# Cross-attention softmax divided on the query rows, and one layer's mask added to the copied scores by GpSimd

## The chip, the cores and the metric

The kernel runs on one core of one Trainium2 chip. Such a core has a TensorE for matrix products, three engines for elementwise work (VectorE or DVE, ScalarE or ACT, GpSimd or POOL) and a SyncE that issues most of the transfers. They share a memory of 128 partitions, SBUF, and the matmuls write into a second one of eight banks, PSUM. Each engine takes its instructions in order and waits at semaphores for the others. The metric is the device time of one execution in microseconds; lower is better.

## The reference, cut to what matters

Two transformer layers on 2 sequences of 1024 rows with 256 columns; each has self-attention, cross-attention to a context of 64 rows, and a feed-forward part. Layer 0's feed-forward is a mixture of 8 experts of which each row takes 2. Layer 1's is dense, and its cross-attention has a mask on the keys. All is float32, with 16 heads of 16 columns. The cross-attention of layer 1 reads:

```python
q = _heads(xn @ q_w.T)
k = _heads(codebook_embeds @ k_w.T)
v = _heads(codebook_embeds @ v_w.T)
attn = jnp.einsum('bhnd,bhmd->bhnm', q, k) * SCALE          # 1024 rows x 64 keys per head
bias = (1.0 - codebook_mask.astype(attn.dtype))[:, None, None, :] * -10000.0
attn = jax.nn.softmax(attn + bias, axis=-1)
ca = _merge(jnp.einsum('bhnm,bhmd->bhnd', attn, v)) @ ca_proj_w.T
x = x + ca
```

Layer 0's has the same form without `bias`. A softmax is: the row's maximum, the difference, the exponential, the sum over the row, and the division by it. The division can be made on the weights or, since the product with v is linear, on the product.

## The kernel before

**Self-attention.** Each layer goes through 128 cells (function `self_attention`). A cell multiplies four tiles of scores of 128x512 with queries on partitions, only for their row maxima (the "a" scores, L801, reduced by DVE at L808), ten cells ahead (`LEAD`), and four with keys on partitions (the "b" scores, L812), which ACT turns into exponentials `pt_s` (L818). Every two cells the product with v follows (L863); ACT copies it (L875) and GpSimd adds it up (L876). So "beside the maxima" below means: while cells with both kinds of scores run. In the last ten cells of a layer there are no "a" scores any more.

**The planner.** All other work is a task, a generator that issues some instructions and yields their estimated TensorE time in us; a yield of zero or less asks for a pause of so many us, which the planner rounds up to cells of 2.9 us, at least one (`Stream.advance`). In each cell the planner takes steps of tasks up to a paced amount. After the last cell, `Stream.rest` orders what is left by rank and by these times. The result fixes the order of instructions on PE, DVE, ACT and SP; GpSimd's order comes from it by way of the scheduler.

**Cross-attention.** The 2048 rows go in four blocks of 512 (`cross_tasks`). For each there are three tasks: `norm`, `weigh`, `share`. `weigh` handles the 16 heads in two groups of eight, and each group in four tiles of 128x512: on the partitions are 128 queries, and in the row four query tiles t, two heads and 64 keys, so that a tile holds 128x8 rows of 64 scores. Its steps are named by two letters:

- SC, `scores`: for two tiles, eight matmuls (L1138), in layer 1 with eight more ahead of them that write the mask into the bank from one row of ones (L1129). Beside the maxima ACT copies the bank to SBUF (`sc_c`, L1149). Otherwise DVE takes maximum and difference straight from the bank.
- LA, `largest`: beside the maxima, DVE's maximum of the copied tile (L1158, 128x8 maxima) and GpSimd's subtraction (L1159).
- TU, `weights_turned`: TensorE transposes two tiles (L1174), and ACT takes the exponential from the bank (`pt_c`, L1178); keys are now on partitions.
- PR, `product`: four matmuls with v (L1187) into one bank; 16 with a matrix of zeros and ones from `picks` into another, which gives the sums over keys (L1197); ACT copies the product to `q_c`, DVE takes the reciprocal of the sums (L1206, 128x128, `inv_c`).
- DI, `divided`: four matmuls spread the reciprocals over the columns of each head (L1212), and DVE multiplies `q_c` by them (L1219).

`share` waits, makes the second DI and projects onto the rows (L433). A step that runs once `maxima[0]` is false, after the last "a" scores, takes the other form: this holds for block 3 and a part of block 2 in layer 0, and for blocks 2 and 3 in layer 1. There the list of steps is written out with a pause for each.

**Around it.** In layer 0 the mixture's dispatch (L1424 and others) runs beside the last cells; expert slots are TensorE work from 590 to 950 us (L1651, L1681), with ACT's Gelu at L1657. Their results leave by indirect transfers (L1696). The last slots are under a run-time condition (`Mixture.others`), at the joint where layer 1's cells begin. The slots' weights (`slotw`) and other tiles (`epool`) lie in pools that are closed at this joint; layer 1's tiles take their places. At the end of layer 1 the feed-forward (L1811, L1823, Gelu at L1814) is all that stands beside the last cross blocks.

Of the kernel before, what the change touches and what calls it, by code (L numbers as in the profile page):

```python
# [50 lines left out]
P = 128  # L51
B, S, D, H, DH = 2, 1024, 256, 16, 16
SK = 64
# [53 lines left out]
O_SUM, O_HEAD = 0, 128  # L107

O_ROWS, O_PART = 640, 704
NPICK = 768  # L110
# [91 lines left out]
def two_blocks(  # L202
# [100 lines left out]
    def other_constants():  # L303
        nc.gpsimd.memset(restart, 1.0)
        nc.gpsimd.memset(restart[:, :, 0:1], 0.0)
        nc.gpsimd.memset(vbds[0], 0.0)

# [214 lines left out]
    def self_attention(layer, tail, heads, arrive, extra, when_ready, beside=None):  # L522
# [379 lines left out]
        if layer == 0:  # L902
# [9 lines left out]
            for _ in first_heads():  # L912
                pass
            stream.add(biases(), 3.3, last=6, mark="biases")
# [183 lines left out]
    def weigh(layer, b, pool, w, name, held):  # L1098
# [24 lines left out]
        def scores(g, n):  # L1123

            got = [(r, *bank()) for r in (2 * n, 2 * n + 1)]
            for t in range(4):
                for r, _, p in got if layer == 1 else ():
                    at = slice(32 * r, 32 * r + 1)
                    nc.tensor.matmul(  # L1129
                        p[:, t * P : (t + 1) * P].rearrange("p (u k) -> p u k", k=SK),  # L1130
                        lhsT=ones[at, :],
                        rhs=mask_f[at, b * SK : (b + 1) * SK].unsqueeze(1).to_broadcast([1, 2, SK]),
                        start=True,
                        stop=False,
                    )
                for r, _, p in got:
# [5 lines left out]
                        start=(layer == 0),  # L1142
# [20 lines left out]

        def largest(g, r):
            if (g, r) in whole_scores:
                subtract(less[g, r], less[g, r], nc.gpsimd, f"{g}{r}")

        def weights_turned(g, n):

            for r in (2 * n, 2 * n + 1):  # L1170
# [7 lines left out]
                nc.scalar.activation(pt, p, AF.Exp, scale=SCALE)  # L1178
                free.append(i)


        inverse = {}

        def product(g):
# [9 lines left out]
            j, s = bank()  # L1194
            for r in range(4):
                for c in range(4):
                    nc.tensor.matmul(  # L1197
                        s[32 * c : 32 * (c + 1), :P],
                        lhsT=picks[:, O_SUM + 32 * r : O_SUM + 32 * (r + 1)],
                        rhs=pts[g, r][:, c * P : (c + 1) * P],  # L1200
                        start=(r == 0),
                        stop=(r == 3),
                    )
            nc.scalar.copy(q[:, g, :], o)
            inv = inverse[g] = pool.tile([P, P], F32, tag="inv", name=f"inv_{name}{g}", bufs=2)
            nc.vector.reciprocal(inv, s[:, :P])  # L1206
            free.extend((i, j))

        def divided(g):
            i, p = bank()  # L1210
            for c in range(4):
                nc.tensor.matmul(  # L1212
                    p[:, c * P : (c + 1) * P],
                    lhsT=picks[:, O_HEAD + c * P : O_HEAD + (c + 1) * P],
                    rhs=inverse[g],
                    start=True,
                    stop=True,
                )
            nc.vector.tensor_tensor(q[:, g, :], q[:, g, :], p, ALU.mult)  # L1219
            free.append(i)  # L1220

        held.update(ot=q, divided=divided)
        cost = 1.9 if layer else 1.0
        SC, LA, TU, PR, DI = scores, largest, weights_turned, product, divided
        if maxima[0]:

            for now, wait in (
                (((SC, 0, 0), (LA, 0, 0)), 0.0),
                (((LA, 0, 1),), 0.0),
                (((SC, 0, 1), (LA, 0, 2)), 0.0),  # L1230
                (((TU, 0, 0), (LA, 0, 3)), 0.0),
                (((SC, 1, 0), (LA, 1, 0)), 0.0),
                (((TU, 0, 1), (LA, 1, 1)), 0.0),
                (((SC, 1, 1), (LA, 1, 2)), 0.0),
                (((PR, 0), (LA, 1, 3)), -1.5),
                (((TU, 1, 0),), None),
                (((DI, 0), (TU, 1, 1)), -1.4),
                (((PR, 1),), None),
            ):
                for step, *args in now:  # L1240
                    step(*args)
                us = sum({SC: cost, TU: 1.15, PR: 1.1, DI: 0.55}.get(step[0], 0.0) for step in now)
                if us:
                    yield us
                if maxima[0]:
                    yield 0.0
                elif wait is not None:
                    yield wait
            return
        for step, *args, wait in (  # L1250
            (SC, 0, 0, None),
            (SC, 0, 1, -1.0),
            (TU, 0, 0, None),
            (SC, 1, 0, None),
            (TU, 0, 1, -1.3),
            (PR, 0, None),
            (SC, 1, 1, None),
            (TU, 1, 0, None),
            (DI, 0, None),
            (TU, 1, 1, -1.6),  # L1260
            (PR, 1, None),
        ):
            step(*args)
            yield {SC: cost, TU: 1.15, PR: 1.1, DI: 0.55}[step]
# [3 lines left out]
    def share(w, name, first, held):  # L1268

        yield -2.6  # L1270
        held["divided"](1)
        yield 0.55
        yield -1.2
# [670 lines left out]
    slotw.append(slots.enter_context(tc.tile_pool(name="slotw", bufs=2, side="right")))  # L1944
    for n in range(2):
        epool.append(
            slots.enter_context(tc.tile_pool(name=f"epool{n}", bufs=2 - n, side="right"))
        )
    mixture.load()
# [31 lines left out]
    def beside(begin):  # L1981
# [4 lines left out]
        both.rest({}, 0)  # L1986
        mixture.others()
# [18 lines left out]
def _layout(inputs):  # L2006
# [84 lines left out]
    for r in range(4):  # L2091
        for u in range(2):
            for c in range(4):
                picks[SK * u : SK * (u + 1), O_SUM + 32 * r + 8 * c + 2 * r + u] = 1.0
# [52 lines left out]
```

## Time and profile before

| | us |
|---|---|
| three runs | 1619.12, 1614.07, 1609.81 |
| their median | 1614.07 |
| the profiled execution | 1624.94 |
| its span in the trace | 1623.2 |
| layer 0's cells | about 54 to 589 |
| layer 1's cells | about 956 to 1462 |

Times are read from the start of the span. A line such as "L1178 ACT ACTIVATE pt_c<-banks 128x512 ... x64 | 35.4, 612 | 22.1 <-PE banks L1174" says: 64 activations at line 1178, from PSUM ("banks") to `pt_c`, busy 35.4 us in all and 612 ns each; ACT stood idle for 22.1 us just before them, mostly until the transposes of L1174 had come. A float32 matmul of the program stands as two records, so that the 16 sum matmuls of a group are 32 of L1197. Matmuls overlap, so their number by their mean may exceed their busy time. In a row of a stretch come its limits and length, then busy time and instructions of each engine, the granted TensorE clock (1.00 is full), the transfers' share and their GB/s. In the chain of waits a row has the time, the duration and the work: it follows the last instruction back to what released each step.

### The profile page before, as it was taken

How to read it: one execution, taken by the hardware profiler on the slowest of the kernel's cores; microseconds unless marked ns; L12 is line 12 of the kernel's file. 1: busy time of each engine (PE TensorE's matmuls, PEld its weight loads, DVE VectorE, ACT ScalarE, POOL GpSimd, SP SyncE). 2: the span in 40 equal slices, each digit the busy share in tenths (PEclk: the TensorE clock that was granted, in tenths of full speed). 3: DMA queues.
4: the chain of work that ended last, by engine and by line, in shares of the span. 5: the costliest groups of instructions: out<-in, count | busy, mean ns of one | idle time of the engine just before them, and what ended most of it. 6: DMA issues, size and time to landing. Idle time of an engine off the chain costs nothing.

```text
span 1623.2 us, 28319 instructions
## 1 busy us (share of the span) xinstructions
PE 1579.5 (97%) x10710; PEld 876.8 (54%) x10710; DVE 985.1 (61%) x2094; ACT 912.9 (56%) x1767; POOL 411.0 (25%) x546
## 2 busy tenths in 40 slices
PE   7999999999998999999999999999999999999998
PEld 3433444544443547878888653344344435546766
DVE  5787776687778647511114457876867767855400
ACT  3487777676665755332233327876776676674321
POOL 2243323144235202311112032411322323311000
PEclk9899999999998999999999999999999999999999
DMA  5235311101000115375556321101110002000000
GB/s 158 112 133 194 111 27 34 28 21 47 14 21 34 54 50 196 102 275 188 186 201 217 92 72 27 33 23 21 34 33 21 22 14 83 15 14 21 14 13 26
DMA packets 55751, 121.07 MB, mean 75 GB/s; under 512 B 12218, under 2 KB 26428, under 8 KB 55228
## 3 DMA queue, kind: packets, MB, share of 16 engines
q1 hardware_dynamic: 51772, 109.07, 20.7%
q0 software_dynamic: 3456, 9.51, 1.6%
q8 instruction: 86, 1.41, 0.4%
q10 hardware_dynamic: 384, 0.66, 0.2%
q14 instruction: 53, 0.43, 0.1%
HBM read 71.68 MB, written 38.88 MB: 68 GB/s over the span
## 4 chain that ended last, share of the span: by engine, by line
PE 89%; DVE 7%; ACT 1%; issue 1%; DMA 1%; another core or an unknown queue 1%; POOL 0%; SPq 0%; DVEq 0%; POOLq 0%; ACTq 0%
PE banks L812 16%; PE banks L801 14%; PE banks L863 13%; PE banks L1651 8%; PE banks L1681 8%; PE banks L631 4%; PE banks L433 3%; PE banks L1823 3%; PE banks L1811 3%; DVE mx_s L808 3%; PE banks L1138 2%; PE banks L601 2%; PE banks L1174 2%; PE banks L1108 2%; PE banks L365 2%; PE banks L709 1%
## 5 line engine op out<-in xcount | busy, mean ns | idle before, releaser
L808 DVE TENSOR_REDUCE mx_s<-banks 128x1 f32<-128x512 f32 x1024 | 634.7, 682 | 215.3 <-PE banks L801 210.3
L818 ACT ACTIVATE pt_s<-banks 128x512 f32<-128x512 f32 x1024 | 532.6, 609 | 155.7 <-PE banks L801 124.8
L801 PE MATMUL banks<-KS,QS 16*128 16x512 f32 x2048 | 537.4, 631 | 4.0 <-DVE count L1441 2.6
L812 PE MATMUL banks<-qb_s,KS 32*128 32x512 f32 x2048 | 517.6, 623 | 6.7 <-DVE qb_s L711 3.7
L876 POOL TENSOR_TENSOR acc_s<-acc_s,part_s 128x512 f32<-128x512 f32 x141 | 179.5, 1273 | 439.0 <-ACT part_s L875 438.3
L812 PEld LDWEIGHTS banks<-qb_s,KS 32*128 32x128 f32 x2048 | 181.0, 187 | 178.5 <-DVE mx_s L808 105.4
L863 PE MATMUL banks<-pt_s,v_s 128*20 128x512 f32 x2048 | 262.0, 603 | 1.5 <-DVE mx_s L808 1.0
L801 PEld LDWEIGHTS banks<-KS,QS 16*128 16x128 f32 x2048 | 200.9, 186 | 76.3 <-issue 37.0
L1681 PE MATMUL banks<-w_slot,h_s 128*128 128x256 f32 x640 | 143.3, 380 | 2.7 <-ACT h_s L1657 2.7
L863 PEld LDWEIGHTS banks<-pt_s,v_s 128*20 128x20 f32 x2048 | 43.0, 98 | 185.0 <-ACT pt_s L818 131.6
L1681 PEld LDWEIGHTS banks<-w_slot,h_s 128*128 128x128 f32 x640 | 120.5, 190 | 22.8 <-ACT h_s L1657 3.1
L875 ACT COPY part_s<-banks 128x512 f32<-128x512 f32 x155 | 92.7, 598 | 61.3 <-PE banks L863 50.6
L1690 DVE SCALAR_TENSOR_TENSOR ys<-banks,gate,b 128x256 f32<-128x256 f32 x40 | 19.3, 483 | 170.3 <-PE banks L1681 163.3
L1657 ACT ACTIVATE h_s<-banks,w_slot 128x256 f32<-128x256 f32 x104 | 43.7, 471 | 109.0 <-issue 61.9
L1651 PE MATMUL banks<-xsT,w_slot 128*128 128x256 f32 x416 | 95.4, 381 | 0.7 <-ACT xsT L372 0.7
L1696 POOL DMA_INDIRECT results<-ys,to x40 | 38.8, 970 | 225.8 <-DVE ys L1690 183.3
L1651 PEld LDWEIGHTS banks<-xsT,w_slot 128*128 128x128 f32 x416 | 77.4, 190 | 14.9 <-DVE mx_s L808 2.3
L1159 POOL TENSOR_TENSOR sc_c<-sc_c,mx_c 128x512 f32<-128x512 f32 x38 | 40.0, 1054 | 98.8 <-DVE mx_c L1158 98.7
L631 PE MATMUL banks<-xT_s,w_att 128*128 128x512 f32 x128 | 63.9, 635 | 0.0
L1814 ACT ACTIVATE h_f<-banks,w_ff 128x512 f32<-128x512 f32 x32 | 22.0, 687 | 73.9 <-PE banks L1811 73.9
L1657 ACT ACTIVATE h_s<-banks,spare 128x256 f32<-128x256 f32 x56 | 23.3, 471 | 63.9 <-issue 30.4
L1823 PE MATMUL banks<-w_ff,h_f 128*128 128x256 f32 x256 | 57.3, 380 | 0.0
(270 smaller groups left out, 1647.2 us busy)
## 6 DMA issues: line engine op xcount, KB each, us to landing
w_slot<-in_ff_w_dram SPq DMA_DIRECT2D x40, 576.0 KB
sorted_rows<-fill SPq DMA_DIRECT2D x36, 520.0 KB
w_slot<-in_ff_w_dram SPq DMA_DIRECT2D x26, 514.0 KB
whole<-acc_s SPq DMA_DIRECT2D x30, 256.0 KB
spare<-in_ff_w_dram SPq DMA_DIRECT2D x14, 514.0 KB
xs<-sorted_rows SPq DMA_DIRECT2D x20, 260.0 KB
y<-results SPq DMA_DIRECT2D x16, 256.0 KB
QS<-stq_s SPq DMA_DIRECT2D x124, 32.0 KB
```

Of the source, the lines that this page charges most:

```text
L631: nc.tensor.matmul(p, lhsT=w[:, at + k * D + pair * P : at + k * D + (pair + 1) * P], rhs=xT[b][:, k, blk * 512 : (blk + 1) * 512], start= ...
L801: nc.tensor.matmul(sc, lhsT=QS[h % 4][r, qc * P : (qc + 1) * P], rhs=K[r, kh * 512 : (kh + 1) * 512], start=True, stop=True,)
L808: return i, lambda: nc.vector.tensor_reduce(mx[h][:, qc, j, kh : kh + 1], sc, AX.X, ALU.max)
L812: nc.tensor.matmul(sc, lhsT=K[r, n * P : (n + 1) * P], rhs=QB[h][r, :], start=True, stop=True)
L818: nc.scalar.activation(pt, sc, AF.Exp, scale=SCALE)
L863: nc.tensor.matmul(o[32 * j : 32 * j + VW, :], lhsT=V[b][:, cell % 8, 4 * g + j, :], rhs=exps.pop((cell, j)), start=(cell == cells[0]), st ...
L875: nc.scalar.copy(part, o)
L876: helper().tensor_tensor(acc[h], acc[h], part, ALU.add)
L1651: nc.tensor.matmul(ph[:, n, :], lhsT=w[:, at : at + P], rhs=xT[:, k, :], start=(k == 0), stop=(k == 1),)
L1657: nc.scalar.activation(h1[:, f, :], ph[:, n, :], AF.Gelu, bias=w[:, W_B1 + f : W_B1 + f + 1])
L1681: nc.tensor.matmul(py, lhsT=h1[:, f, h * P : (h + 1) * P], rhs=w[:, f * D : (f + 1) * D], start=(f == 0), stop=(f == 7),)
L1823: nc.tensor.matmul(py[:, n, :], lhsT=h1[:, f, t * P : (t + 1) * P], rhs=w2[:, f * D : (f + 1) * D], start=(f == 0), stop=(f == 7),)
```

## The change

The exponential moves ahead of the transposes, so that queries are still on partitions when the weights are summed. Four things follow:

- EX, `exponentials`: ACT takes the exponential of a subtracted tile in SBUF, in place. TU's activation becomes a copy.
- DI, `divided`, is another step than before: DVE's sum over each row of 64 keys (128x8 sums), their reciprocals, and the product of tile and reciprocals, by GpSimd beside the maxima and by DVE after them. The matmuls of L1197 and L1212, the reciprocals of 128x128 and the products of L1219 go, and with them a sixth of `picks`. `share` has no DI any more, and waits once.
- MA, `mask`: in layer 1, beside the maxima, the mask is added to the copied scores by GpSimd, ahead of their maximum, and the matmuls of L1129 are left out. After the maxima they stay.
- The order beside the maxima is now computed: one tile per cell, SC every second one; with MA, LA one cell later; EX two cells after LA, DI one after EX, TU and PR behind. It has 15 cells in layer 0 and 17 in layer 1, for 11 entries before. The list for after the maxima has new pauses too.

Two edits lie outside: `epool` is opened before `slotw`, and two activations of one column (`ready_for_exp`) take an exponential ahead of its use, one near the start of layer 0, one ahead of the conditional slots.

```diff
-O_SUM, O_HEAD = 0, 128
-
-O_ROWS, O_PART = 640, 704
-NPICK = 768
+O_HEAD = 0
+
+
+O_ROWS, O_PART = 512, 576
+NPICK = 640
...
+    def ready_for_exp():
+
+        nc.scalar.activation(root, eps, AF.Exp)
+
...
             for _ in first_heads():
                 pass
+            ready_for_exp()
             stream.add(biases(), 3.3, last=6, mark="biases")
...
             got = [(r, *bank()) for r in (2 * n, 2 * n + 1)]
+            masked = layer == 1 and not maxima[0]
             for t in range(4):
-                for r, _, p in got if layer == 1 else ():
+                for r, _, p in got if masked else ():
...
-                        start=(layer == 0),
+                        start=not masked,
...
+        def mask(g, r):
+            if (g, r) in whole_scores:
+                sc = less[g, r].rearrange("p (c k) -> p c k", k=SK)
+                row = mask_f[:, b * SK : (b + 1) * SK].unsqueeze(1).to_broadcast(shape)
+                nc.gpsimd.tensor_tensor(sc, sc, row, ALU.add)
+
         def largest(g, r):
             if (g, r) in whole_scores:
                 subtract(less[g, r], less[g, r], nc.gpsimd, f"{g}{r}")
+
+        def exponentials(g, r):
+            nc.scalar.activation(less[g, r], less[g, r], AF.Exp, scale=SCALE)
+
+        def divided(g, r):
+
+            sc = less[g, r].rearrange("p (c k) -> p c k", k=SK)
+            sm = pool.tile([P, 8], F32, tag="smc", name=f"sm_{name}{g}{r}", bufs=4)
+            nc.vector.tensor_reduce(sm, sc, AX.X, ALU.add)
+            nc.vector.reciprocal(sm, sm)
+            helper().tensor_tensor(sc, sc, sm.unsqueeze(2).to_broadcast(shape), ALU.mult)
 
         def weights_turned(g, n):
...
-                nc.scalar.activation(pt, p, AF.Exp, scale=SCALE)
+                nc.scalar.copy(pt, p)
                 free.append(i)
...
+        costs = {scores: 1.9 if layer and not maxima[0] else 1.0, weights_turned: 1.15, product: 0.55}
...
         if maxima[0]:
...
+            m = layer
+            cells = [[] for _ in range(15 + 2 * m)]
+            for k in range(8):
+                g, r = divmod(k, 4)
+                at = k + (2 + m) * g
+                if r % 2 == 0:
+                    cells[at].append((SC, g, r // 2))
+                    cells[at + 5 + m].append((TU, g, r // 2))
+                if m:
+                    cells[at].append((MA, g, r))
+                cells[at + m].append((LA, g, r))
+                cells[at + m + 2].append((EX, g, r))
+                cells[at + m + 3].append((DI, g, r))
+            for g in range(2):
+                cells[9 + m + (5 + m) * g].append((PR, g))
+            for now in cells:
                 for step, *args in now:
                     step(*args)
-                us = sum({SC: cost, TU: 1.15, PR: 1.1, DI: 0.55}.get(step[0], 0.0) for step in now)
+                us = sum(costs.get(step, 0.0) for step, *_ in now)
                 if us:
                     yield us
...
+                if now is not cells[-1]:
+                    yield 0.0 if maxima[0] else -1.5
             return
...
+        for now, wait in (
+            (((SC, 0, 0),), None),
+            (((SC, 0, 1),), -2.0),
+            (((EX, 0, 0), (EX, 0, 1)), -1.2),
+            (((DI, 0, 0), (DI, 0, 1), (EX, 0, 2), (EX, 0, 3)), -2.4),
+            (((TU, 0, 0), (DI, 0, 2), (DI, 0, 3)), None),
+            (((SC, 1, 0),), -1.6),
+            (((TU, 0, 1),), -1.0),
+            (((SC, 1, 1), (PR, 0)), -1.6),
+            (((EX, 1, 0), (EX, 1, 1)), -1.2),
+            (((DI, 1, 0), (DI, 1, 1), (EX, 1, 2), (EX, 1, 3)), -2.4),
+            (((TU, 1, 0), (DI, 1, 2), (DI, 1, 3)), -2.6),
+            (((TU, 1, 1),), -1.6),
+            (((PR, 1),), None),
         ):
...
     def share(w, name, first, held):
 
-        yield -2.6
-        held["divided"](1)
-        yield 0.55
-        yield -1.2
+        yield -1.4
...
-    slotw.append(slots.enter_context(tc.tile_pool(name="slotw", bufs=2, side="right")))
+
     for n in range(2):
         epool.append(
             slots.enter_context(tc.tile_pool(name=f"epool{n}", bufs=2 - n, side="right"))
         )
+    slotw.append(slots.enter_context(tc.tile_pool(name="slotw", bufs=2, side="right")))
...
         both.rest({}, 0)
+        ready_for_exp()
         mixture.others()
```

More of the change, by code (lines that the diff above doesn't have):

```diff
@@ L1177, in weights_turned @@
                 pt = pts[g, r] = pool.tile([P, 512], F32, tag="p1", name=f"pt_{name}{g}{r}", bufs=4)
-                nc.scalar.activation(pt, p, AF.Exp, scale=SCALE)
+                nc.scalar.copy(pt, p)
                 free.append(i)
-        inverse = {}
         def product(g):
@@ L1193, in product @@
                 )
[L1194 to L1203, printed above, removed]
-            nc.scalar.copy(q[:, g, :], o)
-            inv = inverse[g] = pool.tile([P, P], F32, tag="inv", name=f"inv_{name}{g}", bufs=2)
@@ L1206, in product @@
[L1206 to L1219, printed above, removed]
-            free.append(i)
@@ L1222, in weigh @@
-        held.update(ot=q, divided=divided)
-        cost = 1.9 if layer else 1.0
-        SC, LA, TU, PR, DI = scores, largest, weights_turned, product, divided
-        if maxima[0]:
[L1227 to L1239, printed above, removed]
+            nc.scalar.copy(q[:, g, :], o)
@@ new lines, in product @@
+            free.append(i)
+        held.update(ot=q)
+        costs = {scores: 1.9 if layer and not maxima[0] else 1.0, weights_turned: 1.15, product: 0.55}
+        SC, MA, LA, EX, DI, TU, PR = (
+            scores, mask, largest, exponentials, divided, weights_turned, product
+        )
+        if maxima[0]:
+            m = layer
[14 more added lines that the diff above has]
+            for now in cells:
@@ L1240, in weigh @@
                 for step, *args in now:
                     step(*args)
-                us = sum({SC: cost, TU: 1.15, PR: 1.1, DI: 0.55}.get(step[0], 0.0) for step in now)
+                us = sum(costs.get(step, 0.0) for step, *_ in now)
                 if us:
                     yield us
[L1245 to L1248, printed above, removed]
+                if now is not cells[-1]:
+                    yield 0.0 if maxima[0] else -1.5
@@ L1249, in weigh @@
             return
[L1250 to L1261, printed above, removed]
-        ):
-            step(*args)
-            yield {SC: cost, TU: 1.15, PR: 1.1, DI: 0.55}[step]
+        for now, wait in (
[12 more added lines that the diff above has]
+            (((PR, 1),), None),
+        ):
+            for step, *args in now:
+                step(*args)
+            us = sum(costs.get(step, 0.0) for step, *_ in now)
+            if us:
+                yield us
@@ L2090, in _layout @@
     picks = np.zeros((P, NPICK), f32)
[L2091 to L2094, printed above, removed]
     for j in range(4):
```

## The prediction

> **What bounds the kernel.** I read the page first: busy times, then the chain of waits.
>
> ```profile
> PE 1579.5 (97%) x10710; PEld 876.8 (54%) x10710; DVE 985.1 (61%) x2094; ACT 912.9 (56%) x1767; POOL 411.0 (25%) x546
> ...
> PE 89%; DVE 7%; ACT 1%; issue 1%; DMA 1%; another core or an unknown queue 1%; POOL 0%; SPq 0%; DVEq 0%; POOLq 0%; ACTq 0%
> ```
>
> TensorE is busy for all but 44 us of 1623.2 and carries 89% of the chain. So a TensorE microsecond is worth nearly a microsecond, wherever no other engine is close behind. The stretches of 50 us show how close they are: the first row lies in layer 1's attention with a cross block in it, the second where the last cross blocks run beside the feed-forward (columns: busy PE, PEld, DVE, ACT, POOL).
>
> ```profile
> 1200.00:1250.00 50.00, 49.10 (x420) 25.29 (x416) 36.47 (x61) 33.75 (x66) 13.80 (x12) 1.00 0.07 23
> ...
> 1450.00:1500.00 50.00, 48.73 (x354) 30.79 (x351) 26.34 (x64) 23.76 (x43) 5.85 (x17) 1.00 0.05 17
> ```
>
> Then the groups by shape that the change touches.
>
> ```profile
> L1178 ACT ACTIVATE pt_c<-banks 128x512 f32<-128x512 f32 x64 | 35.4, 612 | 22.1 <-PE banks L1174 21.5 <-ACT pt_c L1178 0.6
> L1129 PE MATMUL banks<-mask_i,ones 1*128 1x128 f32 x256 | 27.5, 281 | 0.0
> L1158 DVE TENSOR_REDUCE mx_c<-sc_c 128x8 f32<-128x512 f32 x38 | 25.6, 673 | 14.7 <-ACT sc_c L1149 14.6
> L1197 PE MATMUL banks<-pt_c,picks 128*32 128x128 f32 x512 | 17.7, 273 | 0.0
> L1212 PE MATMUL banks<-inv_c,picks 128*128 128x128 f32 x128 | 17.6, 280 | 0.3 <-DVE inv_c L1206 0.2 <-DVE mx_s L808 0.2
> L1206 DVE RECIPROCAL inv_c<-banks 128x128 f32<-128x128 f32 x16 | 15.3, 958 | 25.4 <-PE banks L1197 25.4
> L1219 DVE TENSOR_TENSOR q_c<-q_c,banks 128x512 f32<-128x512 f32 x16 | 10.9, 683 | 12.8 <-PE banks L1212 12.8
> L1159 POOL TENSOR_TENSOR sc_c<-sc_c,mx_c 128x512 f32<-128x512 f32 x38 | 40.0, 1054 | 98.8 <-DVE mx_c L1158 98.7
> ```
>
> Last, the chain in two places: a division in layer 0, and the joint where layer 1's attention begins.
>
> ```profile
> 562.49 0.87 PE banks L1197 x32
> ...
> 565.45 0.89 PE banks L1212 x8
> ...
> 950.55 3.36 DMA results<-ys,to
> ...
> 954.31 1.28 ACT L818
> ```
>
> The 32 sum matmuls of 273 ns lie in 0.87 us: they overlap, so I price them by the chain and not by duration times count.
>
> **What the Trainium skill says.** "TensorE: Matmul & The Clock Gate", Part 3, The mechanism: small matmuls at different tile positions run at once; the 0.87 us agrees. "ScalarE: Activation LUTs", What ACT_TABLE_LOAD costs: a switch of function set takes 1283 ns plus a drain of about 1380; the trace has 1283 ns for each load and the next activation 20 ns behind it (load at 1472.08, Gelu at 1473.38), so I take 1.28. "SBUF — State Buffer", Who interferes with whom: a DVE instruction with two SBUF inputs and a GpSimd one that reads SBUF exclude each other, one with a single input doesn't. The added sums have one input; the two-input products on DVE come where GpSimd has little to do (5.85 of 50 us). No row of before isolates the exclusion.
>
> **Removed from TensorE.** Each of 16 divisions (2 layers, 4 blocks, 2 groups) loses L1197 and L1212: 16 x 0.87 + 16 x 0.89 = 28.2 us. The mask of layer 1 stays in blocks 2 and 3, which in the new order have their scores after the row maxima are done, and goes in blocks 0 and 1. L1129's 27.5 us cannot just be halved, since it overlaps L1138: one masked call in the timeline goes from 1457.32 to the next scores at 1458.99, 1.67 us, and two calls without a mask take 1.72 us (layer 0, 628.82 to 630.54), 0.86 each. Eight calls x 0.81 = 6.5 us. Sum 34.7 us.
>
> **The joint.** The slot weights and the other slot tiles swap places in SBUF. In before the first pt_s of layer 1 lie on ys tiles, so ACT's table load waits for the scatter of results (3.36 us of chain), and TensorE stands idle 2.91 us at 953. In the new layout pt_s lies on slot weights, whose readers have ended; the scatter is no longer among that load's waits. The exponentials can start at about 953.2 instead of 955.6: 2.4 us. The preloading of Exp there gains nothing, because the program after the branch carries a load of its own.
>
> **Added, and what hides it.** *DVE*: 64 sums of 0.67, 64 reciprocals of 128x8 (128x32 takes 0.34, 128x4 0.19; I take 0.2), 30 products of 0.69; minus 16 x (0.96 + 0.68). Net 43 + 13 + 21 - 26 = 51 us. In a block beside the maxima it is 8 x 0.87 - 2 x 1.64 = +3.7 us over some 15 to 17 cells of about 4.2 us; DVE rises from 73% (36.47 of 50) to about 78%. Maxima and sums mostly fall in different cells (they meet in three of thirteen), so a cell has 2.48 of L808 plus 0.7 to 0.9. TensorE covers that except in those three and where dispatch is on DVE too: about 1 us a block, 5 us. *ACT*: 64 exponentials in SBUF of 0.6 = 38 us; the old one becomes a copy of equal size. 67% rises to 73%. *GpSimd*: 34 products and 16 mask additions at 1.05 = 53 us. It is 28% busy (13.80 of 50) and reaches about 50% in a block of layer 1, 3.8 us in its fullest cell. An exponential comes two cells after the subtraction that it reads, the transposes one or two cells after GpSimd's product. Against late ones, 34 x 0.15 = 5 us.
>
> *Last blocks.* Here DVE must do max, subtraction, sum, reciprocal and product, 2.9 us a tile. In block 3 of layer 0 the four subtractions end 5.5 us after the first scores, two products 3.1 us later; TensorE has only L1053 (3.6 us) between: about 5 us idle. In layer 1 feed-forward matmuls of 5 to 10 us stand between scores and transposes: nothing, unless ACT is late. Exponentials and Gelu now alternate: the built order has 26 executed table loads for 13, ten of the new ones in layer 1's end. Ten x 1.28 = 13 us on an ACT with 24 of 50 us busy. Eight banks let TensorE run some 10 us ahead; I charge a quarter, 3 us, and keep 0 to 13.
>
> Loads issued by SP keep their order but for one pair of slot weights, taken earlier; picks shrinks by a sixth. Neither is waited for.
>
> Sum: -34.7 - 2.4 + 5 (DVE) + 5 (GpSimd) + 5 (layer 0's last block) + 3 (tables) = -19 us. The profiled execution was 1624.94 us (span 1623.2, 1.7 around it), so 1606. It lies 0.7% above the median of the three runs, 1614.07 (1609.81 to 1619.12); against that median I expect **1595**. Below about 0.5% (8 us) a change cannot be told from none.
>
> **Rivals.**
> 1. *All of it counts* (0.12): no new idle time; -37 us, 1577. For it: ACT, DVE and GpSimd all stay under 80%. Against: the chain already has L808 in 3%, so DVE is not free.
> 2. *DVE takes the gain back* (0.14): cells with a sum become DVE's. All 29 us of sums and reciprocals in the maxima stretches, plus the last blocks' 8, meet a saving of 37: about 0 to -8, 1610. For it, the stretch where block 2 of layer 0 meets dispatch, in which DVE (fourth of the busy times) is already busier than TensorE and GpSimd (sixth) is near:
>
> ```profile
> 505.00:526.00 21.00, 18.37 (x110) 7.32 (x106) 19.01 (x39) 12.06 (x23) 15.47 (x14) 0.83 0.15 52
> ```
>
> Against: of 540 us of layer 0's attention DVE is busy for 396, and no other stretch looks like this one.
> 3. *GpSimd holds up ACT, and so TensorE* (0.20), the slower side. Its queue is in order: accumulation, subtraction, mask and product share it. A late subtraction stops ACT at its exponential; the attention's exponentials behind it keep the banks. A late mask stops DVE at its maximum. With 34 exponentials it decides at 37 / 34 = 1.1 us each; at 1.5 us it costs 51, net +14: 1628. For it: three GpSimd operations per cell at 1.05 to 1.27, and in the stretch above the scatters of dispatch (L1424, 0.96 us each by their median), of which up to five stand ahead of one subtraction in the new order. Against: two cells (8 us) of room.
>
> The likeliest has 0.54. Faster is 0.53 of it plus rival 1, 0.65; rival 2 gives most of 0.15 for the same; slower 0.20. The range reaches from rival 1 to within the slower side, 1578 to 1623, leaving out half of each outer case; the likeliest alone spans 1585 to 1605.
>
> **What would show it.** Right: no L1197 or L1212; L1129 halved; TensorE's busy time down by about 35 us and its idle time up by less than 18; no scatter in the chain at the joint; ACT's added exponentials without long waits on GpSimd. Wrong: idle time of ACT before these, ended by GpSimd's subtraction, above 30 us; the share of L808 in the chain well above 3%; TensorE waiting for GpSimd's or DVE's product before the transposes by more than 20 us; table loads in the chain near the end.

## The result, and the profile after

The changed kernel takes 1636.07 us (median of 4 runs, 1634.16 to 1645.64); the kernel before took 1614.8 us beside it. The ratio is 1.0142, with a 95% interval of 1.0114 to 1.017: it is 1.4% slower where I had forecast 1.2% faster. A second batch on another chip gave 1.0132 (1.0109 to 1.0154). The profiled execution took 1636.58 us, with a span of 1634.8 us.

First the busy times of the page, and the row of the TensorE clock in 40 slices of the span. The first row of the clock is the kernel before, the second the changed one.

```profile
PEclk9899999999998999999999999999999999999999
```

```profile
PE 1567.2 (96%) x9942; PEld 846.4 (52%) x9942; DVE 1037.0 (63%) x2237; ACT 965.4 (59%) x1855; POOL 471.5 (29%) x590
...
PEclk9898999999899998999999999999999999989999
```

The other engines are as priced: DVE +52 us (I had +51), ACT +52.5 (38 and thirteen table loads of 1.28, 55), GpSimd +60.5 (53; a mask addition takes 1.27 us and not 1.05, and ten more accumulations fell to it, L881 x151 for x141). TensorE is the surprise. It has 768 records fewer, and yet is busy for only 12.3 us less, not 35. The view of the cores says why: the mean granted clock fell. Before, then after:

```profile
core 0: 1623.2 us, clock 0.985
```

```profile
core 0: 1634.8 us, clock 0.974
```

The share withheld times the span is 24.3 us before and 42.5 us after (1623.2 x 0.015; 1634.8 x 0.026). By the clock's own records it is 23.9 and 41.9 us, always in stretches at half clock, whose lengths are multiples of 3.41 us up to 17.07 (but for the last one, which the end cuts). Where such a stretch lies over a gap of TensorE it costs nothing; counted only while TensorE was busy, 22.9 us are lost before and 38.1 after, 15.2 more. So the span's difference closes: TensorE's work at full clock fell by 12.3 + 15.2 = 27.5 us, half clock gave back 15.2, and TensorE's idle time rose from 43.7 to 67.6 us, 23.9. That makes +11.6, which is 1634.8 - 1623.2.

What TensorE waits for, the longest rows, changed kernel first, then before (total us, times, longest):

```profile
PE banks L1198 <- POOL sc_c L1190: 12.3, 5, 3.7
PE banks L1198 <- DVE sc_c L1190: 10.9, 8, 6.8
PE banks L370 <- DVE xn_s L358: 9.2, 3, 7.6
```

```profile
PE banks L365 <- DVE xn_s L353: 9.1, 3, 7.5
...
PE banks L1174 <- DVE sc_c L1159: 1.7, 3, 0.6
```

The transposes waited for 1.7 us before. Now they wait for 23.2 us for the product of weights and reciprocals, by GpSimd beside the maxima and by DVE after them. That is nearly all of the new idle time. The groups by shape that answer to those shown of before:

```profile
L1188 DVE TENSOR_REDUCE sm_c<-sc_c 128x8 f32<-128x512 f32 x64 | 43.2, 675 | 8.8 <-ACT sc_c L1182 8.8
L1182 ACT ACTIVATE sc_c<-sc_c 128x512 f32<-128x512 f32 x64 | 40.1, 640 | 6.6 <-DVE sc_c L1166 6.0 <-POOL sc_c L1166 0.6
L1198 PE MATMUL banks<-ident,sc_c 128*128 128x128 f32 x256 | 39.0, 290 | 25.9 <-POOL sc_c L1190 12.3 <-DVE sc_c L1190 10.9 <-DVE mx_s L813 1.8
L1190 POOL TENSOR_TENSOR sc_c<-sc_c,sm_c 128x512 f32<-128x512 f32 x34 | 35.9, 1059 | 32.0 <-DVE sm_c L1189 25.7 <-ACT sc_c L1156 4.1 <-ACT pt_s L823 2.0
L1165 DVE TENSOR_REDUCE mx_c<-sc_c 128x8 f32<-128x512 f32 x36 | 24.0, 666 | 6.0 <-ACT sc_c L1156 3.7 <-POOL sc_c L1175 2.2
L1175 POOL TENSOR_TENSOR sc_c<-sc_c,mask_i 128x512 f32<-128x512 f32 x16 | 20.0, 1272 | 3.9 <-ACT sc_c L1156 3.9
L1136 PE MATMUL banks<-mask_i,ones 1*128 1x128 f32 x128 | 12.5, 282 | 0.0
```

ACT's exponentials waited for GpSimd for 0.6 us in all, and DVE's maxima for the mask for 2.2. Neither of these is where the time went.

One gap in detail, the first block of layer 1. TensorE in order of time, then DVE, then GpSimd (start, duration, work, idle time before it and what ended it):

```profile
1216.46 0.66 PE L1198 MATMUL banks<-ident,sc_c 128*128 128x128 f32 x4
1220.31 1.12 PE L1198 MATMUL banks<-ident,sc_c 128*128 128x128 f32 x4 [3.19 <-POOL sc_c L1190]
```

```profile
1215.26 0.67 DVE L1188 TENSOR_REDUCE sm_c<-sc_c 128x8 f32<-128x512 f32 x1
1215.97 0.20 DVE L1189 RECIPROCAL sm_c<-sm_c 128x8 f32<-128x8 f32 x1
```

```profile
1214.20 1.04 POOL L1166 TENSOR_TENSOR sc_c<-sc_c,mx_c 128x512 f32<-128x512 f32 x1
1216.77 1.26 POOL L509 TENSOR_TENSOR ot_s<-ot_s,by_s 128x512 f32<-128x512 f32 x1 [1.52 <-DMA by_s<-turns]
1217.99 1.26 POOL L881 TENSOR_TENSOR acc_s<-acc_s,part_s 128x512 f32<-128x512 f32 x1
1219.21 2.04 POOL L1190 TENSOR_TENSOR sc_c<-sc_c,sm_c 128x512 f32<-128x512 f32 x2
```

The reciprocals are ready at 1216.17, and TensorE is through with the first tile at 1217.1. GpSimd's next instruction is not the product, though, but self-attention's division of a head group (L509), which stands for 1.52 us at a transfer. It and one accumulation go first. The product starts at 1219.21 and TensorE has stood for 3.19 us. Within the gap, from 1219.8, its clock is halved for 6.83 us.

The stretches shown of before, in the changed kernel. In the first and second the clock falls from 1.00 to 0.93, and TensorE from 49.10 and 48.73 us busy to 46.80 and 47.14. The third is the one on which the rival of DVE rested; its blocks lie a little differently now, and TensorE is busy for 19.97 of 21 us, DVE for 20.31.

```profile
1200.00:1250.00 50.00, 46.80 (x340) 21.34 (x336) 35.94 (x64) 33.16 (x65) 20.55 (x18) 0.93 0.09 28
1450.00:1500.00 50.00, 47.14 (x301) 23.30 (x300) 28.14 (x51) 32.40 (x53) 0.00 (x0) 0.93 0.05 17
505.00:526.00 21.00, 19.97 (x124) 8.33 (x128) 20.31 (x52) 13.80 (x28) 12.85 (x23) 0.92 0.04 14
```

At the joint the scatter of results is out of the chain; what stands there now is the table load that I had expected:

```profile
954.23 1.28 ACT L823
```

To place the rest I cut each trace at the same events: first exponential of a layer, its 257th, the end of its last, the end of the last slot. Two executions of each kernel were profiled (the second ones are described below); the 52 to 55 us ahead of the first cell are left out. The time lost to half clock is half of each stretch, gaps under it included. The chain of the changed kernel covers only its second half, so I compare stages and not chains.

| stage, us | before | changed | idle, before | idle, changed | lost to half clock, before | changed |
|---|---|---|---|---|---|---|
| layer 0, first 64 cells | 256.0, 260.0 | 256.6, 256.7 | 1.0, 1.5 | 1.8, 1.9 | 8.5, 11.9 | 11.9, 11.9 |
| layer 0, second 64 cells, and slots | 640.2, 632.2 | 643.1, 649.9 | 16.5, 10.4 | 25.8, 25.3 | 10.2, 10.2 | 17.1, 23.9 |
| joint, and layer 1's first 64 cells | 252.6, 252.6 | 247.4, 247.6 | 6.3, 6.5 | 4.6, 4.6 | 3.4, 3.4 | 0, 0 |
| layer 1, second 64 cells | 259.9, 260.3 | 273.1, 272.7 | 4.0, 3.8 | 14.9, 15.4 | 0, 1.7 | 11.9, 11.9 |
| end | 160.8, 164.1 | 163.0, 162.8 | 5.4, 5.4 | 10.0, 9.8 | 0, 4.5 | 1.0, 0.8 |

The time is lost in two places: in layer 1 where its blocks 0 and 1 lie, 13 us, and in the second half of layer 0 and its slots, 3 to 18 us by the pair one takes. About 5 us are won at the joint. Of the 11.9 us lost to half clock in layer 1's second 64 cells, 6.8 follow the two gaps of 3.2 and 3.4 us in which TensorE waited for GpSimd's product. The rest does not: a stretch of 3.41 us comes after a wait of 2.3 us for another tile (`xn_c`, L358) at 1439, and one of 6.83 us, from 1462.2, after no gap at all.

### The profile page after: what moved, and what is told of

The parts are those of the page before. It is cut to its first block, busy times and chain, and to the rows that moved or that the text cites. A ratio compares the mean times of both kernels' runs of the same rounds, so it can differ in the third digit from the quotient of the medians.

```text
span 1634.8 us, 27013 instructions
## 1 busy us (share of the span) xinstructions
PE 1567.2 (96%) x9942; PEld 846.4 (52%) x9942; DVE 1037.0 (63%) x2237; ACT 965.4 (59%) x1855; POOL 471.5 (29%) x590
## 5 line engine op out<-in xcount | busy, mean ns | idle before, releaser
L806 PE MATMUL banks<-KS,QS 16*128 16x512 f32 x2048 | 546.3, 638 | 2.0 <-ACT part_s L880 1.8
L817 PE MATMUL banks<-qb_s,KS 32*128 32x512 f32 x2048 | 529.6, 634 | 8.9 <-DVE qb_s L716 3.7
L881 POOL TENSOR_TENSOR acc_s<-acc_s,part_s 128x512 f32<-128x512 f32 x151 | 191.7, 1269 | 407.5 <-ACT part_s L880 406.6
L868 PE MATMUL banks<-pt_s,v_s 128*20 128x512 f32 x2048 | 272.7, 618 | 0.4 <-DVE mx_s L813 0.4
L880 ACT COPY part_s<-banks 128x512 f32<-128x512 f32 x166 | 99.8, 602 | 60.9 <-PE banks L868 48.7
L1198 PE MATMUL banks<-ident,sc_c 128*128 128x128 f32 x256 | 39.0, 290 | 25.9 <-POOL sc_c L1190 12.3
L1813 PE MATMUL banks<-hT_f,w_ff 128*128 128x512 f32 x128 | 57.2, 595 | 0.0
## 6 DMA issues: line engine op xcount, KB each, us to landing
whole<-acc_s SPq DMA_DIRECT2D x30, 256.0 KB
y<-results SPq DMA_DIRECT2D x16, 256.0 KB
```

The lines of the kernel that those rows point to most:

```text
L806: nc.tensor.matmul(sc, lhsT=QS[h % 4][r, qc * P : (qc + 1) * P], rhs=K[r, kh * 512 : (kh + 1) * 512], start=True, stop=True,)
L817: nc.tensor.matmul(sc, lhsT=K[r, n * P : (n + 1) * P], rhs=QB[h][r, :], start=True, stop=True)
L868: nc.tensor.matmul(o[32 * j : 32 * j + VW, :], lhsT=V[b][:, cell % 8, 4 * g + j, :], rhs=exps.pop((cell, j)), start=(cell == cells[0]), st ...
L880: nc.scalar.copy(part, o)
L881: helper().tensor_tensor(acc[h], acc[h], part, ALU.add)
L1813: nc.tensor.matmul(ph, lhsT=w1[:, at : at + P], rhs=hT[:, k, :], start=(k == 0), stop=(k == 1))
```

## The experiments

My theory after the result (A): GpSimd's product comes about a cell late for the transposes, since it stands in a queue with others; each gap of some 3 us then costs about as much again at half clock. The rivals: (B) the added work itself is too much for DVE, ACT and GpSimd together; (C) half clock has nothing to do with the gaps. All ratios are to the kernel before, run beside it on the same chip. Between batches chips differ: the kernel before took 1629.08 us on the first batch's, 1617.06, 1615.02 and 1616.1 on the others'. So between batches I go by stages. The changed kernel was not run on the first batch's chip. The stage that the first four edits hardly touch, the joint and layer 1's first 64 cells, takes 246.9 to 248.3 us there and 247.4 and 247.6 in the changed kernel, so its stages can be compared; why the kernel before was 13 us slower on that chip stays open.

**Transposes one cell later.** Beside the maxima, in both layers.

```diff
-                at = k + (2 + m) * g
+                at = k + (3 + m) * g
-                    cells[at + 5 + m].append((TU, g, r // 2))
+                    cells[at + 6 + m].append((TU, g, r // 2))
-                cells[9 + m + (5 + m) * g].append((PR, g))
+                cells[10 + m + (6 + m) * g].append((PR, g))
```

> The changed kernel with each transpose and product one cell later beside the maxima, and the second group one cell later. Theory A (TensorE stands before the transposes because GpSimd's product ends about one cell late, and each such gap of 2 to 4 us is followed by half clock): the wait for GpSimd's product falls from 12.3 us to under 4, half clock in layer 1's second 64 cells from 12.0 us lost to under 4, and the time from 1636 to 1612 to 1622. Theory B (the sum of the added work on DVE, ACT and GpSimd lengthens the cells, whatever the order): 1632 to 1640. Theory C (half clock comes by itself, not from gaps): waits fall, the lost clock stays near 43 us over the kernel, 1625 to 1630.

1617.54 us, ratio 0.9911 (0.988 to 0.9942). The wait for GpSimd:

```profile
PE banks L1198 <- POOL sc_c L1190: 1.8, 1, 1.8
```

Layer 1's second 64 cells, as one row each: before, changed, and here (TensorE's clock is the third from the end).

```profile
1202.40:1462.30 259.90, 255.87 (x2186) 122.90 (x2183) 186.39 (x331) 181.62 (x352) 69.72 (x105) 1.00 0.09 29
```

```profile
1198.70:1471.80 273.10, 258.16 (x1877) 111.04 (x1870) 197.83 (x371) 192.85 (x374) 105.94 (x126) 0.96 0.08 27
```

```profile
1202.90:1442.60 239.70, 237.14 (x1790) 104.31 (x1787) 188.36 (x359) 186.28 (x364) 103.27 (x124) 1.00 0.09 31
```

GpSimd is as busy as in the changed kernel, 103 for 106 us, and no gap is left above 1.5 us. The clock is full throughout. Some work moved from here into the end (174.5 us for 163.0); both together take 414.3 us for 436.1, a gain of 22, of which 15 are idle time. So B falls in layer 1: the same work, ordered one cell later, leaves less idle time in these cells (2.6 us) than the kernel before had (4.0). For C something remains: over the whole kernel 37.7 us are still lost to half clock, for 41.9, since the end now has two stretches of 6.83 us, from 1463.2 and 1521.3, with no gap over 1.2 us ahead of them. In layer 0 there was no gain: its second 64 cells and slots took 646.5 us. TensorE now waits for 3.8 us for sorted rows of the slots, which come out of the last cross block by way of dispatch: a later block ends later.

**The product by DVE.**

```diff
-            helper().tensor_tensor(sc, sc, sm.unsqueeze(2).to_broadcast(shape), ALU.mult)
+            nc.vector.tensor_tensor(sc, sc, sm.unsqueeze(2).to_broadcast(shape), ALU.mult)
```

> The changed kernel with the 34 products of weights and reciprocals made by DVE instead of GpSimd. Theory A: no product stands in GpSimd's queue, so the 12.3 us of wait for it go, at 0.69 us of DVE each in cells that have some room: 1615 to 1628. Theory B: DVE is the engine that lengthens the cells, 34 x 0.69 = 23 us more on it: 1640 to 1655.

1645.22 us, ratio 1.0089 (1.0066 to 1.0112). The absolute time lies in B's range, but on the chip where the kernel before took 1629.08 us; the ratio is not above the changed kernel's on its own chips (1.0142 and 1.0132). So this run does not decide for B, and there is more in it than a sum of durations. The durations of the products (min, median, max in ns):

```profile
L1190 DVE TENSOR_TENSOR sc_c<-sc_c,sm_c x64: 691/693/3999, 270.4 to 1566.8; 128x512 f32<-128x512 f32 x64
```

The median is unmoved and one takes 4.0 us, from 405.94 to 409.94; GpSimd worked without a pause until 409.38. All 64 take 53.3 us in place of 44.4. Of the changed kernel's 30 on DVE, after the maxima, all take about 0.69. The page "SBUF — State Buffer", Who interferes with whom, of the Trainium skill says that a DVE instruction with two SBUF inputs and a GpSimd one that reads SBUF exclude each other; these longer products beside a busy GpSimd agree with it. Layer 1's second cells and end still gained 3.6 us (432.5 for 436.1), while layer 0's second half and slots took 656.8, with 25.6 us lost to half clock.

**Self-attention's division by DVE**, so that GpSimd does not stand at that transfer.

```diff
-        helper().tensor_tensor(dst, dst, by, ALU.mult)
+        nc.vector.tensor_tensor(dst, dst, by, ALU.mult)
```

> The changed kernel with self-attention's own division of a head group (line 509, 1.26 us on GpSimd, waiting there for a transfer) made by DVE, so that GpSimd's queue no longer stands at that transfer. If it is this one instruction that the product is queued behind, the gaps near 1217 and 1352 us (3.2 and 3.4) go with their half clock of 3.4 us each, and the time falls to 1618 to 1626. If GpSimd is late without it too, 1632 to 1638. DVE may stand at the transfer in its place: then slower than 1640.

1627.11 us, ratio 0.9985 (0.9967 to 1.0003). The two gaps of 3.2 and 3.4 us in layer 1 are gone, and the one of 3.7 us near 409 in layer 0 is 2.0; the wait for GpSimd's product fell from 12.3 to 4.8 us, and layer 1's second cells and end from 436.1 to 426.8 us. So this one instruction ahead in the queue made the two gaps of layer 1. In the slots, though, this run had a gap of 11.6 us before the transposes of layer 0's block 3, where the changed kernel had 6.8 (below).

**The mask by TensorE again.**

```diff
-            masked = layer == 1 and not maxima[0]
+            masked = layer == 1
...
-                if m:
-                    cells[at].append((MA, g, r))
```

> The changed kernel with layer 1's mask multiplied by TensorE in all four blocks, as before, and no additions on GpSimd. TensorE gets 8 x 0.8 = 6.5 us back. If the 16 additions of 1.25 us make GpSimd late (part of theory A), the gaps in layer 1 shrink and the time is 1620 to 1632. If they have room, the work counts alone: 1640 to 1645.

1636.15 us, ratio 1.0053 (1.0037 to 1.0069). Layer 1's second cells and end take 435.8 us, the changed kernel's 436.1 and 435.5. The wait for GpSimd's product fell from 12.3 to 8.9 us, and TensorE's added work took it back. So in this order the mask's move neither made the loss nor saved the 6.5 us that I had entered for it.

**The blocks after the maxima in the form of before.**

```diff
+        held.update(ot=q, divided=None if whole else spread_sums)
...
+        TU, PR, DI = turned_exp, product_sums, spread_sums
+        for step, *args, wait in (
+            (SC, 0, 0, None),
+            (SC, 0, 1, -1.0),
+            (TU, 0, 0, None),
...
```

> The changed kernel in the blocks beside the maxima, but the blocks after the maxima (block 3 of layer 0, blocks 2 and 3 of layer 1) in the form of before: exponential after the transposes, sums and spreading by TensorE, the old list of pauses. If the last blocks cost what their stages show (6.4 us more idle time between layer 0's cells and the joint with 3.4 us more lost to half clock, and an end that is not shorter although TensorE has 3.4 us less work in it), the stage from layer 0's last cell to the joint goes back from 368 to about 361 us and the ratio to before from 1.014 to about 1.008. If the last blocks were hidden work, TensorE only gets six divisions back, 6 x 1.76 = 10.6 us, and the ratio rises to 1.020.

1626.66 us, ratio 1.005 (1.0034 to 1.0065): nearly a point of the loss is gone, more than expected. Layer 0's second 64 cells and slots take 631.6 us for 643.1 and 649.9. In the changed kernel, DVE has to take the first tiles of layer 0's block 3 through maximum, subtraction, sum and product while TensorE has nothing else to do: a gap of 6.8 us at 627, and 13.65 us at half clock from 629.3, of which 9.0 lie behind the gap and cost 4.2. In the three runs just above the gap was 11.6 us, and DVE had stood, ahead of its maxima, for 2.4 to 3.8 us at something that the profile names only "remote". That stays open. Layer 1's second cells and end took 438.1 us for 436.1: there the old form gains nothing. The ten table loads that the new form brings to that end, which I had priced at 3 us, cost 1.7 us at most in the changed kernel: two stand in its chain, and TensorE waits once for the Gelu behind the second, which it did not do before.

```profile
1549.01 1.28 ACT L1182
...
1555.93 1.28 ACT L1816
```

```profile
PE banks L1825 <- ACT h_f L1816: 1.7, 1, 1.7
```

**The pools swapped, alone**, in the kernel before.

```diff
-    slotw.append(slots.enter_context(tc.tile_pool(name="slotw", bufs=2, side="right")))
     for n in range(2):
         epool.append(
...
+    slotw.append(slots.enter_context(tc.tile_pool(name="slotw", bufs=2, side="right")))
```

> The kernel before with only the two pools of slot tiles opened in the other order. If the joint's 2.9 us gap comes from the scatter of results on whose place the first exponentials lie, it goes, with the 3.4 us of half clock after it: 4 to 6 us faster, ratio 0.996 to 0.9975. If the place does not matter, within 2 us of before.

1615.45 us, ratio 0.9984 (0.9973 to 0.9995), a gain of 0.8 to 4.4 us: less than I had expected of it, but a gain. The joint takes 4.0 us for 5.9, and layer 1's first 64 cells, now at full clock, 244.6 for 246.8.

**No division at all**, in the kernel before.

```diff
-            j, s = bank()
-            for r in range(4):
-                for c in range(4):
...
-            inv = inverse[g] = pool.tile([P, P], F32, tag="inv", name=f"inv_{name}{g}", bufs=2)
...
-            nc.vector.tensor_tensor(q[:, g, :], q[:, g, :], p, ALU.mult)
```

> The kernel before with the division of the cross-attention left out (no sums, reciprocals, spreading or product; everything else stays). It bounds what taking the division from TensorE can give: 16 x 1.76 = 28 us if each TensorE microsecond counts, ratio 0.983. If a part was waited out anyway, or gives new gaps with half clock, 0.988 to 0.995.

1588.92 us, ratio 0.9809 (0.9779 to 0.9839): 26 to 36 us, 28.1 between the medians, and 28.2 were priced. The division that the change takes from TensorE was sized rightly and is worth its full time.

**Later transposes and old last blocks.** The edits of the first and the fifth experiment.

> Both edits: transposes one cell later beside the maxima, and the blocks after the maxima in the form of before. By the sum of the first at 0.991 and what the last blocks are thought to cost (about 10 us), 0.985; if the last blocks were hidden, 0.997.

1620.64 us, ratio 1.0013 (0.9998 to 1.0028): the parts did not add. In layer 1 the second cells and the end take 420.3 us, 16 less than in the changed kernel but 6 more than with its own form of the last blocks, which is therefore the better one there. Layer 0's second half and slots took 649.9 us, with

```profile
PE banks L1675 <- DMA xs<-sorted_rows: 8.9, 1, 8.9
```

Blocks that end later hold up dispatch and the slots, and that takes back what the old form of the last block gains.

**The changed kernel again**, to see its spread.

> The changed kernel unaltered, on the chip of this batch, so that the others are read against it and the spread of its stages between two profiled executions is seen. Ratio to before 1.011 to 1.017; in layer 1's second 64 cells about 273 us again, of which about 15 idle and 12 lost to half clock.

1637.83 us, ratio 1.0132 (1.0109 to 1.0154). Its stages are the second numbers in the table above. Layer 1's are the same to 0.4 us; layer 0's second half differs by 7 us, nearly all of it in half clock.

**The gap filled.** In layer 1, three matmuls whose results are not used, ahead of the transposes that wait.

```diff
+                if layer == 1 and (g, r) == (0, 1) and maxima[0]:
+                    for _ in range(3):
+                        nc.tensor.matmul(p, lhsT=ident, rhs=q[:, 0, :], start=True, stop=True)
```

> The changed kernel with three idle matmuls (results unused, about 2.7 us) ahead of the transposes of the second tile in each of layer 1's two blocks beside the maxima, where TensorE stood for 3.2 and 3.4 us. They remove no wait and add work. If the gap is what sets half clock, the two stretches of 6.8 us at half clock behind them go, and layer 1's second 64 cells fall from 273 to about 266 us, ratio 0.4% below the unaltered one. If half clock comes by itself, the stage stays at 273 or grows.

1633.91 us, ratio 1.0127 (1.0103 to 1.0152); over the whole time that cannot be told from the changed kernel. The stage tells it:

```profile
1196.80:1462.60 265.80, 255.48 (x1884) 111.47 (x1880) 197.90 (x372) 192.48 (x374) 106.02 (x126) 0.99 0.09 28
```

265.8 us for 273.1 and 272.7. TensorE does some 5 us more work and is busy for less, as both stretches at half clock behind the filled gaps are gone. Of 11.9 us lost, 3.4 are left, in the stretch that follows no gap (now from 1453.4). That excludes C for these two gaps: nothing else was removed, and the product still starts 3.2 us after its reciprocals do. It does not exclude C for the stretches without a gap.

**The parts that paid.** Transposes one cell later in layer 1 alone, layer 0's block 3 in the form of before, layer 1's last blocks in the new one.

```diff
-                at = k + (2 + m) * g
+                at = k + (2 + 2 * m) * g
-                    cells[at + 5 + m].append((TU, g, r // 2))
+                    cells[at + 5 + 2 * m].append((TU, g, r // 2))
...
+        if layer == 0:
+            TU, PR, DI = turned_exp, product_sums, spread_sums
```

> The changed kernel with the transposes one cell later in layer 1 only, and layer 0's block after the maxima in the form of before. Stages: layer 0 as in the run with the last blocks of before (second 64 cells and slots together 632 us for 643), layer 1's second half and end as in the run with later transposes (414 us for 436). Together about 33 us less than the changed kernel: 0.984 to 0.993 of the kernel before. If the parts do not add, 0.997 or more.

1598.81 us, ratio 0.9907 (0.9882 to 0.9932): faster than both kernels. Stages: 633.1 us for layer 0's second half and slots, 409.4 for layer 1's second cells and end.

**The same, with self-attention's division by DVE.**

> The same with self-attention's division of a head group by DVE too, which took 5 us off the first 64 cells of layer 0 and 9 off layer 1 in its own run. Where layer 1's wait is already gone only the first counts: 3 to 8 us below the same kernel without it.

1599.92 us, ratio 0.9907 (0.9891 to 0.9924). Nothing gained. The first 64 cells of layer 0 took 249.5 us for 252.5, but the end had 8.6 us lost to half clock for 2.5.

**The kernel before again.**

> The kernel before unaltered. Its first profiled execution had gaps of 2.9 and 2.7 us among layer 0's slots that the run with only the pools swapped did not have. If these belong to that one execution, layer 0's second 64 cells and slots take 628 to 634 us here in place of 640, and layer 1's second 64 cells and end 421 us as in both.

1615.95 us, ratio 0.9998 (0.9985 to 1.0012). Layer 0's second half and slots took 632.2 us: the two gaps were that one execution's, and 8 us of the 640.2 with them. So the execution that my sums were made against hid a part of what the change costs in layer 0. The end, on the other hand, took 164.1 us for 160.8: half clock at 1504.4, with no gap ahead of it.

**Later in layer 0 too, but not in its block 2.**

```diff
+            w1 = 1 if layer or int(name[-1]) < 2 else 0
-                at = k + (2 + m) * g
+                at = k + (2 + m + w1) * g
-                    cells[at + 5 + m].append((TU, g, r // 2))
+                    cells[at + 5 + m + w1].append((TU, g, r // 2))
```

> The kernel made of parts, with the transposes one cell later in layer 0's blocks 0 and 1 too, not in block 2. If the lateness of GpSimd's product is the cause in layer 0 as well, the gap of 3.7 us near 408 and the half clock behind it (6.8 us) go, and the ratio falls from 0.991 to 0.984 to 0.988. If any block of layer 0 that ends later makes its last work late (the wait for sorted rows of 3.8 to 8.9 us seen where all three were shifted), it is 0.995 or more.

1594.69 us, ratio 0.9867 (0.9826 to 0.9907), the lowest of the kernels that do the whole computation, though its interval overlaps those of the two made of parts. Layer 0's second half and slots take 626.3 us for 633.1. The gap of 3.7 us near 408 is gone; one of 1.6 us is left there, in which TensorE waits for DVE's row maxima, and the half clock fell from 13.65 to 3.41 us. TensorE does not wait for sorted rows. One long wait for GpSimd's product is left, at 540:

```profile
PE banks L1197 <- POOL sc_c L1189: 4.3, 2, 4.2
```

GpSimd's queue is not what this product waited for last: GpSimd itself stands for 1.22 us just before it, until DVE's sum and reciprocal have come. DVE was held up ahead of that sum by a small operation of dispatch. Below are DVE and GpSimd in this run, and last the same operation in the changed kernel:

```profile
538.35 3.62 DVE L1556 TENSOR_TENSOR begin<-nt,begin 128x8 f32<-128x8 f32 x1
...
542.16 0.68 DVE L1187 TENSOR_REDUCE sm_c<-sc_c 128x8 f32<-128x512 f32 x1
```

```profile
543.15 1.39 POOL L1189 TENSOR_TENSOR sc_c<-sc_c,sm_c 128x512 f32<-128x512 f32 x1 [1.22 <-DVE sm_c L1188]
```

```profile
620.89 0.17 DVE L1475 TENSOR_TENSOR begin<-nt,begin 128x8 f32<-128x8 f32 x1
```

It has two inputs in SBUF and takes 3.62 us in place of 0.17. GpSimd worked without a pause from 537.45 to 541.93, and the operation ended at 541.97. That is the pattern of the one long product by DVE above; no run took it away, so the cause is not shown here.

## Why the prediction was wrong

*Removed from TensorE, 34.7 us.* Right in the main. The division is worth 26 to 36 us where I had 28.2. The 6.5 us of the mask did not show as time. TensorE's work at full clock fell by 27.5 us.

*The joint, 2.4 us.* The mechanism was right. The joint's stage fell by 1.6 us, and the half clock that had followed its gap, 3.4 us, went as well; I had not counted that.

*DVE beside the maxima, 5 us.* Not the place of the loss: the "b" scores waited for DVE's maxima for 2.5 us (1.6 before).

*GpSimd, "the transposes one or two cells after GpSimd's product. Against late ones, 34 x 0.15 = 5 us".* This step failed. The waits are 12.3 us in five places, more than twice that, and each of the three over 3 us has half clock behind it: 6.8 us lost in layer 1 and 5.1 near 414 in layer 0. I counted the distance in cells of the order written down, and only up to the end of the sums. I did not write out what stands between the sum and the product in GpSimd's own queue: L509, which waits there for a transfer, and the accumulations. In before, GpSimd's subtraction came two to four cells ahead of the transposes that read it, so lateness in that queue had no row to show itself in. One cell more, and the wait is 1.8 us.

*Layer 0's last block, 5 us.* The mechanism was right and the size wrong: a gap of 6.8 us (11.6 in some variants) and 4.2 us lost at half clock behind it. With the old form, 357.7 us pass from layer 0's last cell to the end of the slots, for 367.8 and 370.8.

*Tables, 3 us.* All 26 loads were executed. In layer 1's end they cost 1.7 us at most; two of them in the chain there are a sign that I had given.

*Half clock.* This step failed too: it has no term in my sum, and it took 15.2 us more of TensorE's busy time. The page of the Trainium skill that I had cited for packed matmuls, "TensorE: Matmul & The Clock Gate", says in Part 1, What's actually happening, that the clock is halved after an idle window of about 3.4 us and comes back after a busy one. The trace of before had shown it (2.91 us idle at 953.3, then 6.83 us at half clock); I saw the gap and priced only the gap. The runs agree with the page in the size: stretches are multiples of 3.41 us. In the sixteen traces, their first 50 us left out, half clock set in during or within 8 us behind each of the 24 gaps over 3.2 us, 7 of the 9 between 2.9 and 3.2, and 12 of the 30 between 2.0 and 2.9. It also came without a gap, as the last section tells.

Of the rivals, the third had the right engine and the right side. It named the exponentials and the maxima as the ones that would wait for GpSimd; they waited for 0.6 and 2.2 us. What it took to lose was not 1.1 us per exponential, but five late products, three of them with half clock behind, one bare block, and half clock in other places. The sign that I had given for this, transposes waiting for the product by over 20 us, is what came: 23.2 us.

## What to carry to other kernels

When work moves from TensorE to an engine that serves it, write out that engine's queue between the last input and the result, transfers included, and leave a cell more than the sum of durations asks for. A gap on TensorE of 3 us or more was paid twice here, once as a gap and once as the half clock behind it, 3.4 us for a stretch of 6.83. Where TensorE has other work the new form pays; where it has none, as in layer 0's last block, the old form, slow but on TensorE, was better, so the two are chosen block by block.

## What was not expected of the hardware

Adding matmuls made a stage shorter: with some 5 us of unused work in two gaps, layer 1's second 64 cells took 265.8 us for 273. Half clock also came without any gap: in the kernel before, at 1504.4 us for 6.83 us, in its second profiled execution and not in the first, after 3 us of one-row and 32-row matmuls (L1129, L1138) without a pause. The changed kernel has 6.83 us of it within 4 us of such matmuls in both of its executions, from 1462.2 and 1472.2 us, 3.4 us lost each time. What sets it there was not tried.

A small operation held up a chain that seemed to hang on another engine: one of 128x8 took DVE 3.62 us for 0.17 while GpSimd worked without a pause, and the list of waits put TensorE's 4.2 us down to GpSimd's product.
